# Values by seven half products instead of eight, with position copies, normalization and sums moved, in a two-layer attention kernel

## The chip, the cores and the metric

The kernel runs on one core of a Trainium2 chip. The metric is the device time of one execution in microseconds (us). Before the change it is 3358.13 us, the median of three runs (3357.68 to 3358.46).

A core has five engines that run side by side and meet through semaphores: PE (TensorE, matrix products into PSUM; its weight loads are listed as PEld), DVE (VectorE), ACT (ScalarE), POOL (GpSimd) and SP (SyncE, here only a queue that starts DMAs). Each engine works through its own instructions in order.

## The reference

Two layers, each on four images of 32 x 32 positions with 768 channels, 12 heads of 64:

```python
for layer in (0, 1):
    y = group_norm(x, groups=32)            # over positions and 24 channels
    q, k, v = heads(y @ Wqkv + bqkv)        # no bias in layer 0
    bias[h, w, k] = q . Rh  and  q . Rw     # relative positions, along rows and columns
    attn = softmax(scale * q k^T + bias)    # 1024 x 1024 per head
    x = x + (attn @ v) @ Wproj + bproj
```

Everything is float32. For one image the values are one product of a 1024 x 768 matrix (positions by channels) with a 768 x 768 matrix.

## The kernel before

**Units.** There are 8 (layer, image) rounds of 6 head pairs: 48 pairs, numbered g, `pair = g % 6`. A pair is worked in 8 steps n, one for each block of 128 query positions; a step is an iteration of the loop at L776. "Even" and "odd" are said of `pair`. Heads of a pair lie in the two halves of the 128 partitions, and most products use 64 partitions, so that two of them run in PE at the same time.

**One step.** The order of all instructions is written out by hand (`tc.manual_schedule`, L722); each engine's queue is that order cut to its own instructions. A step (g, n) issues: touches for half-done groups (see below); DMAs put off from earlier steps; `biases` two steps ahead (POOL, two passes of 1024 elements); `scores` one step ahead (PE, 8 records), then `exponentials` (DVE subtracts bias from score and takes the minimum, ACT exponentiates); the place copies of the positions; reading back transposed blocks (SP); then products of the next pair, `turn` (two DVE transposes and a store `td` to DRAM), `divide` one step ahead (DVE reciprocal, then ACT, in steps 2 and 4 half on POOL), and further products. In steps 6 and 2 `weigh` multiplies read-back attention blocks (`pt`) with values (`av`, 64 records); DVE copies the sum out.

**Groups of products.** Products of pair g + 1 run during the steps of pair g: G0 to G3 for queries and keys, V0 and V1 for values, O0 and O1 for the output projection. The plan at L769 says which are worked in which step; a group listed in two steps is done in two halves. `crossed` (L315) is such a group: in its first half each of two PSUM banks collects one partition half's products, in its second half the other's. Between them stands `between` (L311), one DVE instruction that rewrites one weight column, so that the second half waits for it and it for the first half. A group's results wait in PSUM in one of two buffers of pool `ps_m`; positions, weighted sums and output products use the same two.

**Queries and keys** are already computed by seven half-size products in place of eight: `combine` (L130) makes differences of weight blocks on POOL, `sums` (L282) differences of input blocks, and G0 to G3 the products, whose results are added by DVE.

**Values** come for two pairs at once (`project_values`, L392): for a double pair starting at an even g, four groups i of 256 positions, each by 24 matmuls with 256 output columns (both pairs' values), and ACT copies the results into the value tiles (L405), two copies a group. Groups 0 and 1 run in the odd pair before, 2 and 3 in the even pair itself. `combine_values` makes one weight difference that the input sums call for.

**Positions.** `positions` (L409) multiplies q with the position table (tile `tp`, 128 columns), ACT copies the result twice (L425, L428); it is called in step 2 and step 7, `place_positions` after the exponentials.

**Next image.** In pair 3 `norm` gathers the statistics and makes scale and shift through small DMAs (steps 1, 2, 4, 5, 7); `applies` says in which steps of pair 4 ACT normalizes which input blocks, `sum_steps` in which steps POOL makes the input sums.

Of the kernel before, what the change touches and what calls it, by code (L numbers as in the profile page):

```python
# [31 lines left out]
FP = mybir.dt.float32  # L32
AF = mybir.ActivationFunctionType
ALU = mybir.AluOpType
ENGINES = {getattr(mybir.EngineType, e) for e in ("PE", "DVE", "Activation", "Pool", "SP")}

P = 128
# [19 lines left out]
def attention_blocks(ctx: ExitStack, tc: tile.TileContext, a: dict, out: bass.AP):  # L57
# [63 lines left out]
    def load_wv(g):  # L121

        im, pair = divmod(g, NP)
        w = wpool.tile([P, NC, 2 * P], FP, tag="wv", name=f"wv_{g}")
        wv_of[g] = w
        nc.sync.dma_start(
            out=w, in_=a[f"wv{images[im][0]}"][pair // 2].rearrange("p (c o) -> p c o", c=NC)
        )
# [11 lines left out]

    def combine_values(g):

        w = wv_of[g]
        nc.gpsimd.tensor_tensor(w[:, NB:], w[:, NB:], w[:, :NB], ALU.subtract)

# [91 lines left out]
    def norm(im):  # L237
# [6 lines left out]
        back = dram2.tile([C, 2], FP, tag="back", name=f"back_{im}")  # L244
        g = small.tile([NG, 2, GS, 2], FP, tag="g", bufs=1, name=f"g_{im}")
        st = small.tile([NG, 2, 6], FP, tag="gst", bufs=1, name=f"gst_{im}")
# [6 lines left out]

        def by_group():
            queue.dma_start(out=g[:, 0, :, :], in_=per.rearrange("(g k) s -> g k s", k=GS))

        def groups():
            for k in range(2):
                nc.vector.bn_stats(st[:, k, :], g[:, 0, :, k])
                nc.vector.bn_aggr(mv[:, k, :], st[:, k, :])  # L260
            nc.vector.tensor_scalar(mv[:, 2, 0:1], mv[:, 0, 1:2], mv[:, 1, 0:1], EPS, ALU.add, ALU.add)
            nc.scalar.activation(mv[:, 2, 1:2], mv[:, 2, 0:1], AF.Sqrt)

        def inverses():
            nc.vector.reciprocal(mv[:, 2, 0:1], mv[:, 2, 1:2])
            nc.vector.tensor_scalar(mv[:, 2, 1:2], mv[:, 0, 0:1], mv[:, 2, 0:1], -1.0, ALU.mult, ALU.mult)
            for k in range(2):
                nc.vector.tensor_copy(g[:, 1, :, k], mv[:, 2, k : k + 1].to_broadcast([NG, GS]))
            queue.dma_start(out=back.rearrange("(g k) s -> g k s", k=GS), in_=g[:, 1, :, :])
# [31 lines left out]
    class Crossed:  # L301
# [8 lines left out]

        def between(self):  # L311
            x = self.last[:, 0:1]
            nc.vector.tensor_reduce(x, x, mybir.AxisListType.X, ALU.max)  # L313

    def crossed(t, pairs, two, kept=None):  # L315

        n = len(pairs)
        for half in range(2):
            for at in range(n):
                for h in range(2):  # L320
                    h = h ^ half
                    rows = ROWS[h ^ half]
                    to, w, x = two(t, pairs[n - 1 - at if half else at], h, rows)
                    nc.tensor.matmul(  # L324
                        to, lhsT=w, rhs=x, start=(half, at) == (0, 0), stop=(half, at) == (1, n - 1)
                    )
            if half == 0:
                yield kept if kept is not None else two(t, pairs[n - 1], 1, slice(0, P))[1]

# [61 lines left out]

    def project_values(g, i):  # L392

        im, pair = divmod(g, NP)
        xn, w = xn_of[im][i // 2], wv_of[g]
        if i == 0:
            for h in range(2):
                v_of[g + h] = vpool.tile([P, NT, P], FP, tag="v", name=f"v_{g + h}")
        t = ps_m.tile([P, 2, HALF], FP, tag="m", name=f"pv_{g}_{i}")
        yield from crossed(t, range(NC), lambda t, c, k, rows: (  # L400
            t[:, k, : 2 * P], xn[c][rows, (2 * (i % 2) + k) * P : (2 * (i % 2) + k + 1) * P],
            w[rows, c, :],
        ), w[:, NC - 1, :])
        for h in range(2):
            nc.scalar.copy(v_of[g + h][:, 2 * i : 2 * i + 2, :], t[:, :, h * P : (h + 1) * P])  # L405
        if i == 3 and g + 2 < NPAIR:
            later.append(lambda: load_wv(g + 2))

# [258 lines left out]
    def run(todo):  # L667
        while todo:
            todo.pop(0)()

    def prepare(g):

        first, i = (g - 1, 2) if g % 2 else (g, 0)
        groups = {f"G{kind}": Crossed(lambda kind=kind: products(g, kind)) for kind in range(4)}
        for k in range(2):
            groups[f"V{k}"] = Crossed(lambda k=k: project_values(first, i + k))
        return groups
# [15 lines left out]
    def take(groups, n):  # L693
# [15 lines left out]
    applies = {  # L709
        2: ((0, 0), (0, 1), (0, 2)), 3: ((0, 3),), 4: ((0, 4), (0, 5), (1, 0)),  # L710
        5: ((1, 3), (1, 1), (1, 4)), 7: ((1, 2), (1, 5)),
    }
    sum_steps = {
        (4, 5): ((3, 0),),
        (4, 6): ((1, 0), (2, 0), (3, 1)),
        (4, 7): ((1, 1), (2, 1)),
        (5, 0): ((3, 2), (1, 2), (2, 2)),
        (5, 1): ((4, 0),),
        (5, 2): ((4, 1), (4, 2)),
    }  # L720

    with tc.manual_schedule(engines=ENGINES):  # L722
# [16 lines left out]
        def both(*names):  # L739
            for name in names:  # L740
                now[name].part()
            for name in names:
                now[name].between()
            for name in names:
                now[name].part()
# [3 lines left out]
        run(placing)  # L749
        both("V1", "G1")  # L750
        later.pop(0)()
        combine_values(0)
        load_w(1, "a")
        now["G2"].part()
        now["G3"].part()
        now["G2"].between()
        now["G2"].part()
        positions(0, 1)()
# [9 lines left out]
        held = [ahead["G0"]]  # L768
        plan = {  # L769
            0: ("O1 previous", "G0", "V0"), 1: ("V0", "V1"), 3: ("V1", "G1"),  # L770
            4: ("G1", "G3", "G2"), 5: ("G2", "O0"), 7: ("O0", "O1", "G0 next"),
        }
        before = {}

        units = [(g, n) for g in range(NPAIR) for n in range(NT)]
        for at, (g, n) in enumerate(units):  # L776
# [37 lines left out]
            if at + 2 < len(units):  # L814
                biases(*units[at + 2])
            placing = [positions_of() for positions_of in (early_positions if n == 2 else ())]
            if n == 2:
                early_positions.clear()
            exps = scores(*units[at + 1]) if at + 1 < len(units) else None
            if n == 7 and g + 1 < NPAIR:  # L820
                placing.append(positions(g + 1, 1))
            if exps:
                exps()
            run(placing)
            run(behind[0])
            behind.append(behind.pop(0))
            if pair == 3 and n in stages and not end:
                stages[n]()
            pieces = [now[name] for name in plan.get(n, ()) if now.get(name)]
            if n == 0 and len(pieces) == 2:  # L830
# [11 lines left out]
            turn(g, n)  # L842
            run_part(1 if n == 0 else len(pieces))
            if at + 1 < len(units):
                divide(*units[at + 1])
            if n in (0, 1) and g + 1 < NPAIR:
                combine(g + 1, n)
            if n == 4 and pair % 2 and g + 1 < NPAIR:
                combine_values(g + 1)
            if pair == 4 and not end:  # L850
                for h, c in applies.get(n, ()):
                    apply(c, h)
            if not end:
                for which, c in sum_steps.get((pair, n), ()):
                    sums(im + 1, which, c)
            for k in range(2 if n == 0 else 1, len(pieces)):
                run_part(k)
# [68 lines left out]
```

## Time and profile before

| | value |
|---|---|
| median of three runs | 3358.13 us |
| the profiled execution | 3358.64 us |
| its span, first to last instruction | 3356.7 us |
| granted PE clock | 0.999 |
| L324 PE value products, 4608 records | mean 376 ns each |
| L420 PE position products, 1536 records | mean 272 ns each |
| L405 ACT value copies, 192 | 59.9 us, 361 ns each |
| L144 POOL value weight difference, 24 | 44.0 us, 1835 ns each |
| L133 POOL weight differences, 192 | some 1000 ns each |
| L313 DVE touches of wv, 96 | 13.9 us, 144 ns each |
| POOL sc waits for DVE tb | 603.7 us, 160 times |

A row of groups gives the line, the engine, the operation, the tile written and the tiles read, the shapes, the count, the busy time and the mean of one. A row in order of time gives the start, the length, and what ran. A row of waits gives who waited for whom, the total, how often, and the longest. Durations of single matmuls include their way through the array, so neighbours overlap; the time between the starts of two runs tells what a run costs. Idle time of an engine that nobody waits for costs nothing.

### The profile page before, as it was taken

What the parts mean: (1) busy time and instruction counts of PE and PEld (TensorE: products, weight loads), DVE (VectorE), ACT (ScalarE), POOL (GpSimd) and SP (SyncE); (2) the same over time, 40 slices, a digit from 0 to 9 for tenths busy, and PEclk for the clock granted to TensorE, in tenths of its full rate; (3) what the DMA queues carried; (4) which work ended last, traced back from release to release, by engine and by line L of the source; (5) the groups of instructions that cost most, each with busy time, mean ns of one, the idle gap of its engine ahead of it and who ended that gap; (6) DMA issues with size and microseconds to landing.
All of it is one profiled execution on the core that took longest, in us unless ns stands there. A gap on an engine that the chain in (4) does not pass through costs nothing.

```text
span 3356.7 us, 58091 instructions
## 1 busy us (share of the span) xinstructions
PE 3316.0 (99%) x21604; PEld 1874.7 (56%) x21604; DVE 2417.8 (72%) x3923; ACT 2041.0 (61%) x3140; POOL 2333.9 (70%) x1187
## 2 busy tenths in 40 slices
PE   6999999999999999999999999999999999999998
PEld 4555555555555555555555555555555555555554
DVE  4887777777787776777777776767776676767775
ACT  3666655566556665566656666566666566665563
POOL 6777866668666686667867668676686667766662
PEclk9999999999999999999999999999999999999999
DMA  3998989899899988998988999999988989898887
GB/s 129 319 331 311 331 308 335 315 327 327 318 323 319 324 315 309 317 326 312 324 310 314 329 313 324 312 326 313 329 311 309 328 309 334 305 319 299 311 290 270
DMA packets 524153, 1046.94 MB, mean 312 GB/s; under 512 B 139104, under 2 KB 202080, under 8 KB 474720
## 3 DMA queue, kind: packets, MB, share of 16 engines
q1 hardware_dynamic: 470976, 1015.84, 85.8%
q10 hardware_dynamic: 52896, 27.40, 2.7%
q8 instruction: 171, 2.80, 0.3%
q14 instruction: 110, 0.90, 0.1%
HBM read 568.00 MB, written 475.09 MB: 311 GB/s over the span
## 4 chain that ended last, share of the span: by engine, by line
PE 95%; DMA 3%; DVE 1%; issue 0%; ACT 0%; SPq 0%; POOL 0%; ACTq 0%; DVEq 0%
PE pj L324 21%; PE av L547 19%; PE s L482 19%; PE pv L324 15%; PE oo L324 13%; PE pj L352 3%; PE tp L420 3%; DMA td<-tb 2%; PE o L626 1%; DMA xn<-in_x 1%; DVE tb L518 1%; DMA pt<-td 1%; DVE st L201 0%; DVE sc L494 0%; POOL sc L468 0%
## 5 line engine op out<-in xcount | busy, mean ns | idle before, releaser
L468 POOL TENSOR_TENSOR sc<-rel 128x1024 f32<-128x1024 f32 x768 | 1880.1, 2478 | 634.9 <-DVE tb L518 603.7
L494 DVE CUSTOM_DVE_ANT_0 sc<-s,sc 128x1024 f32<-128x1024 f32 x768 | 911.1, 1226 | 531.2 <-PE s L482 464.0
L498 ACT ACTIVATE sc<-sc,sm 128x1024 f32<-128x1024 f32 x768 | 878.8, 1146 | 498.2 <-DVE sm L494 497.2
L512 ACT ACTIVATE sc<-sc,sm 128x1024 f32<-128x1024 f32 x674 | 743.0, 1143 | 564.8 <-DVE sm L506 437.5
L518 DVE STREAM_TRANSPOSE tb<-sc 128x1024 f32<-128x1024 f32 x768 | 909.9, 1227 | 36.7 <-DMA td<-tb 35.2
L482 PE MATMUL s<-k,q 64*128 64x512 f32 x3072 | 738.6, 596 | 2.7 <-DVE sm L494 2.7
L547 PE MATMUL av<-pt,v 128*64 128x256 f32 x6144 | 685.3, 381 | 6.5 <-DMA pt<-td 5.5
L547 PEld LDWEIGHTS av<-pt,v 128*64 128x64 f32 x6144 | 434.4, 137 | 286.6 <-issue 44.0
L324 PE MATMUL pv<-wv,xn 64*128 64x256 f32 x4608 | 522.8, 376 | 1.0 <-DVE wv L313 1.0
L324 PEld LDWEIGHTS pv<-wv,xn 64*128 64x128 f32 x4608 | 446.9, 187 | 114.2 <-issue 54.5
L324 PE MATMUL oo<-attn,wo 64*128 64x512 f32 x2112 | 475.3, 589 | 0.0
L482 PEld LDWEIGHTS s<-k,q 64*128 64x128 f32 x3072 | 289.2, 187 | 316.2 <-issue 291.7
L324 PEld LDWEIGHTS oo<-attn,wo 64*128 64x128 f32 x2112 | 200.9, 187 | 228.0 <-issue 227.1
L510 POOL TENSOR_SCALAR sc<-sc,sm 128x1024 f32<-128x1024 f32 x94 | 105.5, 1122 | 303.2 <-DVE sm L506 298.2
L324 PE MATMUL pj<-xn,wa 64*128 64x512 f32 x1152 | 268.1, 596 | 4.4 <-DVE wa L313 2.9
L324 PE MATMUL pj<-xn,w 64*128 64x512 f32 x1152 | 263.3, 589 | 1.6 <-DVE w L313 1.6
L324 PE MATMUL pj<-s,w 64*128 64x512 f32 x576 | 262.5, 589 | 0.0
L324 PE MATMUL pj<-s,wc 64*128 64x512 f32 x576 | 262.5, 589 | 0.0
L324 PEld LDWEIGHTS pj<-xn,wa 64*128 64x128 f32 x1152 | 113.4, 189 | 140.3 <-issue 126.6
L324 PEld LDWEIGHTS pj<-xn,w 64*128 64x128 f32 x1152 | 111.6, 187 | 137.4 <-issue 134.9
L443 ACT COPY rel<-raw 32x256 f32<-32x256 f32 x384 | 155.1, 404 | 16.2 <-DMA rel<-tdr 5.5
L324 PEld LDWEIGHTS pj<-s,wc 64*128 64x128 f32 x576 | 107.7, 187 | 67.4 <-issue 67.4
(86 smaller groups left out, 2127.1 us busy)
## 6 DMA issues: line engine op xcount, KB each, us to landing
td<-tb SPq DMA_DIRECT2D x384, 1024.0 KB, 6.1
pt<-td SPq DMA_DIRECT2D x382, 1024.0 KB, 8.9
tdr<-t ACTq DMA_DIRECT2D x96, 256.0 KB, 6.1
part<-res SPq DMA_DIRECT2D x84, 256.0 KB, 4.2
res<-part SPq DMA_DIRECT2D x84, 256.0 KB, 4.8
wa<-in_wqk SPq DMA_DIRECT2D x48, 384.0 KB, 3.2
wc<-in_wqk SPq DMA_DIRECT2D x48, 384.0 KB, 5.6
wv<-in_wv SPq DMA_DIRECT2D x24, 768.0 KB, 12.5
```

Of the source, the lines that this page charges most:

```text
L324: nc.tensor.matmul(to, lhsT=w, rhs=x, start=(half, at) == (0, 0), stop=(half, at) == (1, n - 1))
L352: nc.tensor.matmul(t[:, h, :], lhsT=w[rows, c, :], rhs=x[c][rows, :], start=(c == 0), stop=(c == NB - 1),)
L420: nc.tensor.matmul(ps[:, h, j, :], lhsT=q[rows, at * P : (at + 1) * P], rhs=tabs[l][rows, :], start=True, stop=True,)
L443: nc.scalar.copy(rel[rows, :, 0, :, :], raw[rows, :, :, WIDE - 1 - HW - y : WIDE - 1 - y])
L468: nc.gpsimd.tensor_tensor(sc.rearrange("p (a k) (u l) -> p a (k u) l", a=4, l=8), rel[:, h, 0, m, :].unsqueeze(1).unsqueeze(3).to_broadcas ...
L482: nc.tensor.matmul(ps[h][:, cols], lhsT=q[rows, n * P : (n + 1) * P], rhs=k[rows, cols], start=True, stop=True,)
L494: nc.vector.tensor_tensor_reduce(out=sc, in0=ps[h], in1=sc, scale=-scale, scalar=BIG, op0=ALU.add, op1=ALU.min, accum_out=st[:, 0, h : h + 1],
L498: nc.scalar.activation(sc, sc, AF.Exp, bias=st[:, 0, h : h + 1], scale=-1.0, accum_out=st[:, 1, h : h + 1],)
L510: nc.gpsimd.tensor_scalar(sc, sc, st[:, 2, h : h + 1], 1.0, ALU.mult, ALU.mult)
L512: nc.scalar.mul(sc, sc, st[:, 2, h : h + 1])
L518: nc.vector.transpose(tb[:, :, h, :], sc_of[g, n, h])
L547: nc.tensor.matmul(av[rows, at * 2 * P : (at + 1) * 2 * P], lhsT=v_of[g][:, k, rows], rhs=pt_of[g, quarter].rearrange("p n r k h i -> p (n ...
```

## The change

Values of a double pair are made by seven half-size products. The value weights are cut into four blocks (by channel half and by pair), the inputs into four (by channel half and by position half). Group kind 0 multiplies raw weights with the first position half; POOL then replaces blocks by differences, in two stages, and kinds 1 to 3 use these with the input sums that queries and keys use already. Kinds 0, 1 and 2 are crossed groups of 48 matmuls with 128 output columns, kind 3 a single part of 24. Results are added up in the value tiles: one ACT copy and nine DVE additions a double pair. Kinds 0 and 3 run in the odd pair, 1 and 2 in the even one, and the plan differs between them: in odd pairs V1 (kind 3) stands after G1 in step 3. The position copies of step 2 go to the end of step 1, ahead of the division there. In step 3 of even pairs the touch is an ACT copy ahead of the division. Normalization and input sums start one step earlier, and the group statistics lie in the buffer of the position copies.

```diff
-    def combine_values(g):
-        w = wv_of[g]
-        nc.gpsimd.tensor_tensor(w[:, NB:], w[:, NB:], w[:, :NB], ALU.subtract)
+    def combine_values(g, stage):
+        w, t2 = wv_of[g]
...
+        if stage == 0:
+            sub(w11, w12, w11)
+            sub(w12, w22, w12)
+        else:
+            sub(t2, w22, w11)
+            sub(w21, w21, t2)
...
+            window = tmppool.tile([P, 2, 4, WIDE], FP, tag="raw", name=f"g_{im}")
...
-        def between(self):
+        def between(self, scalar=False):
             x = self.last[:, 0:1]
+            if scalar:
+                nc.scalar.copy(x, x)
+                return
...
-        t = ps_m.tile([P, 2, HALF], FP, tag="m", name=f"pv_{g}_{i}")
-        yield from crossed(t, range(NC), lambda t, c, k, rows: (
-            t[:, k, : 2 * P], xn[c][rows, (2 * (i % 2) + k) * P : (2 * (i % 2) + k + 1) * P],
-            w[rows, c, :],
-        ), w[:, NC - 1, :])
-        for h in range(2):
-            nc.scalar.copy(v_of[g + h][:, 2 * i : 2 * i + 2, :], t[:, :, h * P : (h + 1) * P])
+        t = ps_m.tile([P, 2, 4, P], FP, tag="m", name=f"pv_{g}_{kind}")
+        if kind == 3:
+            for b in blocks:
+                for c in range(NB):
+                    for h, rows in enumerate(ROWS):
+                        nc.tensor.matmul(
+                            t[:, h, b, :], lhsT=s4[c][rows, b * P : (b + 1) * P], rhs=w22[rows, c, :],
...
+            ops = {
+                0: ((w11, x0), (w21, x0[NB:])),
+                1: ((w2, s2), (w12, s3)),
+                2: ((w11, x1), (w21, x1[NB:])),
+            }[kind]
+            yield from crossed(t, [(b, c) for b in blocks for c in range(NB)], lambda t, bc, h, rows: (
+                t[:, h, bc[0], :], ops[h][1][bc[1]][rows, bc[0] * P : (bc[0] + 1) * P],
+                ops[h][0][rows, bc[1], :],
+            ), 2)
...
+        if kind == 0:
+            nc.scalar.copy(y10, ts[0])
+            add(y00, ts[1], y10)
+        elif kind == 3:
+            add(y01, ts[0], y10)
+            add(y01, ts[1], y01)
+        elif kind == 1:
+            add(y11, ts[0], y10)
+            add(y01, ts[0], y01)
+            add(y11, ts[1], y11)
+        else:
+            add(y10, ts[1], y11)
+            add(y01, ts[0], y01)
+            add(y11, ts[0], y11)
...
-        2: ((0, 0), (0, 1), (0, 2)), 3: ((0, 3),), 4: ((0, 4), (0, 5), (1, 0)),
-        5: ((1, 3), (1, 1), (1, 4)), 7: ((1, 2), (1, 5)),
+        1: ((0, 0), (0, 3)), 2: ((0, 1), (0, 4)), 3: ((1, 0), (1, 1), (0, 2)),
+        4: ((1, 3), (1, 4), (0, 5)), 5: ((1, 2), (1, 5)),
...
-        both("V1", "G1")
+        both("G1", "G2")
         later.pop(0)()
-        combine_values(0)
+        for stage in range(2):
+            combine_values(0, stage)
         load_w(1, "a")
-        now["G2"].part()
         now["G3"].part()
-        now["G2"].between()
-        now["G2"].part()
+        now["V1"].part()
...
-        plan = {
-            0: ("O1 previous", "G0", "V0"), 1: ("V0", "V1"), 3: ("V1", "G1"),
-            4: ("G1", "G3", "G2"), 5: ("G2", "O0"), 7: ("O0", "O1", "G0 next"),
-        }
+        same = {
+            0: ("O1 previous", "G0", "V0"), 4: ("G1", "G3", "G2"), 5: ("G2", "O0"),
+            7: ("O0", "O1", "G0 next"),
+        }
+        plans = {**same, 1: ("V0", "V1"), 3: ("V1", "G1")}, {**same, 1: ("V0",), 3: ("G1", "V1")}
...
+            done = 2 if n == 0 else len(pieces) if n == 1 or (n, pair % 2) == (3, 0) else 1
+            for k in range(1, done):
+                run_part(k)
+            if n == 1:
+                placing = [positions_of() for positions_of in early_positions]
+                early_positions.clear()
+            if (n, pair % 2) == (3, 0):
+                for group in held:
+                    group.between(scalar=True)
+                held = []
             if at + 1 < len(units):
                 divide(*units[at + 1])
...
-            if n == 4 and pair % 2 and g + 1 < NPAIR:
-                combine_values(g + 1)
+            if n in (3, 5) and pair % 2 and g + 1 < NPAIR:
+                combine_values(g + 1, n // 4)
```

## The prediction

> **What bounds the kernel now.** I read the page's engine line first, then the answer for three stretches of the span, then who made TensorE (PE) wait, then its groups by shape and one stretch in order of time.
>
> ```profile
> PE 3316.0 (99%) x21604; PEld 1874.7 (56%) x21604; DVE 2417.8 (72%) x3923; ACT 2041.0 (61%) x3140; POOL 2333.9 (70%) x1187
> ```
> ```profile
> 233.00:3271.00 3038.00, 3036.62 (x19966) 1718.96 (x19966) 2207.38 (x3580) 1884.93 (x2901) 2147.72 (x1081) 1.00 0.90 318
> 0.00:233.00 233.00, 204.03 (x1316) 121.17 (x1316) 159.33 (x269) 127.41 (x203) 163.50 (x98) 0.99 0.73 251
> ```
> ```profile
> PE groups L216 <- DVE nrm L215: 15.0, 1, 15.0
> PE av L547 <- DMA pt<-td: 5.5, 5, 1.7
> PE pj L324 <- DVE wa L313: 2.9, 2, 2.3
> ```
> ```profile
> 1003.81 2.76 PE L324 MATMUL pv<-wv,xn 64*128 64x256 f32 x24
> 1006.40 1.88 PE L482 MATMUL s<-k,q 64*128 64x512 f32 x8
> 1008.12 5.35 PE L324 MATMUL pv<-wv,xn 64*128 64x256 f32 x48
> 1013.30 1.06 PE L420 MATMUL tp<-tab,q 64*128 64x128 f32 x16
> 1014.19 1.89 PE L482 MATMUL s<-k,q 64*128 64x512 f32 x8
> 1016.00 7.13 PE L547 MATMUL av<-pt,v 128*64 128x256 f32 x64
> ```
> From 233 to 3271 us PE is busy 3036.62 of 3038.00 us at full clock (the columns after the length are PE, PEld, DVE, ACT and POOL busy, clock, DMA share, GB/s). So the time is PE's own work plus a head and a tail, and any change must be priced in PE time and in new PE waits. DVE, POOL and the DMA engines (share 0.90) come next and matter only where they make PE wait.
>
> **The unit of PE work.** Each fp32 matmul leaves two records, and matmuls on the two halves of the partitions run at the same time; two concurrent records are one slot below. The time from the start of one run to the next gives its price: 24 records of 256 columns take 1006.40 - 1003.81 = 2.59 us, 12 slots of 216 ns; 16 records of 128 columns (the position products, the only ones of that width) take 1014.19 - 1013.30 = 0.89 us, 8 slots of 111 ns, say 111.5. All of these load new weights in every slot, as the new products do.
>
> **Part 1, the values.** Per double pair (two head pairs) four groups of 24 matmuls of 256 columns go: 96 slots x 216 = 20.74 us. Three groups of 48 and one of 24 matmuls of 128 columns come: 168 slots x 111.5 = 18.73 us. That is 2.01 us less of the bounding engine, all of it in the odd pair (three runs of 24 slots in place of four of 12), while each of the four runs in the even pair grows from 2.59 to 2.68 us. Times 23 double pairs in the loop: -46.2 us. The slot price is bounded below by half of the 216 ns slot (108: -60 us). Above, it is less sure: a slot is four PE records (two weight loads, two matmuls), 28 ns each at 111.5, and the trace holds that pace for 8 slots only, where the new runs have 24 to 48 slots plus the position products. Its longest dense stretches (the 256-column runs) go at 54 ns a record, which would make a slot 216 ns and the kernel 168 x 216 - 20.74 = +15.5 us a double pair, +373 us. I take 111.5, since the eight slots are evenly paced also where PE had waited just before (the position products at 55.1 us).
>
> The Trainium skill ("TensorE: Matmul & The Clock Gate", Back-to-back issue gap) speaks against the change here: a steady stream of weight load and matmul pairs, it says, is held to about 81 ns per matmul at 128 columns, more than the columns alone. By it a slot of two would be 162 ns and the change an estimated +6.5 us a double pair, +155 us; the trace's row beside it is 111 ns for the same kind of slot, in runs of 8.
>
> **Part 2, what follows the products.** ACT loses 8 copies of 361 ns and gains one of 585 per double pair. DVE gains 9 adds of 512 elements from PSUM, at 0.69 us (the row of the same add for k): 6.2 us a double pair, 149 us in all, 72% to some 78%; one DVE touch of 0.14 us a double pair goes. PE pays only where it waits for them. The rows:
> ```profile
> 1009.58 1.22 DVE L494 CUSTOM_DVE_ANT_0 sc<-s,sc 128x1024 f32<-128x1024 f32 x1
> 1010.72 2.37 DVE L518 STREAM_TRANSPOSE tb<-sc 128x1024 f32<-128x1024 f32 x2
> 1013.01 0.12 DVE L506 RECIPROCAL sm<-sm 128x2 f32<-128x2 f32 x1
> ```
> Even pair, step 1: the first value group ends at 1010.97 (24 slots from 1008.12, plus the last one's 0.27), three adds end near 1013.0, and the position products, which take the freed PSUM buffer, are due at 1013.48 after the second group's 24 slots. 0.4 us to spare: 0; without that second group the full 2 us would show. Odd pair, step 1: the copy waits on ACT for the exponentials (they end 4.0 us after the second slot run begins, 943.40 in the pair before) and the add follows, to 944.7; the buffer's next user is the weighted sum at 944.9: 0 to 0.2. Even pair, step 3: three adds, 1.9 us, now stand before the transposes, and the next scores' subtraction is due 0.4 us after the reciprocal: 0, or 0.5 late where statistics (0.9 us) stand there too, and hidden by the 2.57 us of k products. Odd pair, step 3: two adds end with the next scores' arrival: 0. Also there, value kind 3 takes a PSUM buffer between G1 and G3, which costs G3 a wait for two adds (1.6 us, 24 times: +38) if the buffer just freed is given out, and nothing if the older one is. In the old stretch the second value group follows the first without a gap though the copies out of the first end at 1012.73, so the older is given out: 0.
>
> What the DVE adds do delay is the transposes of steps 1 and 3, by some 2.1 to 2.7 us, and on SP's queue everything behind their store:
> ```profile
> 1029.88 0.33 SPq L520 DMA_DIRECT2D td<-tb  x1
> 1030.32 8.67 SPq L454 DMA_DIRECT2D rel<-tdr  x8
> 1039.08 0.38 SPq L119 DMA_DIRECT2D wa<-in_wqk  x1
> 1039.56 0.93 SPq L529 DMA_DIRECT2D pt<-td  x2
> 1040.58 0.46 SPq L520 DMA_DIRECT2D td<-tb  x1
> ```
> ```profile
> DMA to landing us min/median/max: 5.1/8.9/12.8
> ```
> The second read-back lands at about 1040 + 8.9 = 1048.9 and is wanted halfway through the weighted sum, 1051.7. 2.1 us later leaves 0.7 us at the median and a wait of 3.2 at the slowest landing: 0 to 2.1 a pair, I take 0.2. Then the store behind it (1040.58) is late as well, and the transposes two steps on wait for its landing (35.2 us, 22 times, now); behind them on DVE stands the copy that frees the buffer of the next position products, about 1 us ahead of need (1055.95 to 1057.05). 0 to 1 a pair, I take 0.15. Both together: 24 x 0.35 = +8 us, bounds 0 and +50 (24 x 2.1).
>
> **Part 3, the moves.** The position copies go ahead of a division in ACT's queue. The weight load of the weighted sum waits for them 34.9 us in 46 times now, but PE's own list has no such wait, so it gains 0; the division behind them (ACT, one of 1.14 us) waits for the later reciprocal anyway. One touch per even pair moves from DVE to ACT (0.2 us, behind the exponentials, ahead of a division that is not due yet): 0. Combining the value weights: one POOL pass of 1.84 us becomes four of 1.0, in two later steps with several us of POOL idle before the next biases: 0; if POOL were late, the scores' subtraction would be, by up to 1 us. Normalization (12 ACT passes of 0.80 us an image) and sums (12 on POOL of 1.28) start a step earlier, the scale's read having been issued 37 us before its first use now (711.79 to 748.92), still some 28 after: 0, at most 1 us in 7 images. The window that shares the position buffer makes its small read on SP wait for the place copies, with a transposed store queued behind it: under 1 us, 7 times, off the path: 0.
>
> **The head.** From 33.78 to 55.12 us PE does value, query and key groups with two waits (1.58 and 1.17 us) before the second position products. New: four half groups of 2.57, G3 2.57 and kind 3 at 2.68 = 15.5 against 21.3 us, less 0.5 for the wider even runs: -5.3 if nothing else is late. POOL's combine is 2.2 us longer there and the first read-backs already hold PE up: bounds -5.5 and 0, I take -3.
>
> **Sum.** Profiled execution 3358.64 (span 3356.7 and 1.9 around it); -46.2 - 3 + 8 = 3317.4. The median of the runs is 0.5 below the profiled one: 3317.
>
> **Rivals.**
> A, on the other side: PE cannot be fed 128-column slots for that long. For it: no row shows more than 8 in a row. Against: the even pace of those 8, also after a wait. It decides at a slot price of 20.74 / 168 = 123 ns; at 54 ns a record it ends at 3358.6 + 373 = 3732, halfway (164 ns) at about 3525. Chance 0.14.
> B: DVE's lateness is paid in full in each even pair, through the read-back or the buffer: 3317 - 8 + 50 = 3359, or half of it, 3335. For it: the 0.7 us left over; against: a PE wait lets the transfers catch up, and in most pairs the landing is at the median. Chance 0.15, split evenly around 3351.
> C: no new wait, and the whole head: 3358.6 - 46.2 - 5.3 = 3307. Chance 0.06.
> Forecast as summed, 3303 to 3335: 0.65.
>
> **How the numbers follow.** A measurement tells about 0.2%, 6.7 us, from no change. Faster: 0.65 + 0.06 + half of B, 0.08 = 0.79. Same: 0.05 of B and near A's threshold. Slower: 0.16. Range 3302 to 3365: it takes in C's 3307, the forecast and B's 3359, and leaves A out (0.14).
>
> **What would show it.** Right: value matmul records 8064 in place of 4608, mean 272 ns, a 24-slot run near 2.68 us; PE still 99% busy; DVE up by some 145 us and ACT down by some 45. Wrong: value runs of 48 records longer than 2.9 us (A); PE waiting for pt<-td or a value add, or ACT's position copy, some 24 times and by over 1 us (B). The prediction falls if PE's idle time in the loop passes 20 us.

## The result, and the profile after

| | before | after |
|---|---|---|
| median of the runs compared | 3358.3 us (3357.68 to 3359.33) | 3317.65 us (3316.78 to 3318.15) |
| the profiled execution | 3358.64 us | 3317.58 us |
| its span | 3356.7 us | 3315.3 us |
| granted PE clock | 0.999 | 0.999 |

The changed kernel takes 0.9878 of the time before (95% interval 0.9861 to 0.9895), four runs of each. The forecast was 3317.

First the engine line of the page of the changed kernel, and two stretches of its span, the head and the loop (start and end, length; busy time and instructions of PE, PEld, DVE, ACT, POOL; clock; DMA share; GB/s).

```profile
PE 3270.6 (99%) x25060; PEld 1882.7 (57%) x25060; DVE 2549.7 (77%) x4091; ACT 1999.1 (60%) x2996; POOL 2386.5 (72%) x1259
```

```profile
0.00:233.00 233.00, 205.26 (x1646) 126.41 (x1648) 173.87 (x288) 128.94 (x197) 173.01 (x106) 0.99 0.74 262
233.00:3230.00 2997.00, 2990.35 (x23096) 1721.76 (x23092) 2325.17 (x3728) 1841.84 (x2763) 2191.18 (x1145) 1.00 0.91 321
```

PE is still the bound: in the loop it is idle 6.65 of 2997 us, where it was idle 1.38 of 3038. DVE has gained 132 us and ACT lost 42, as the sum had it to within 13 and 3 us.

The waits of PE (who waited for whom, total us, times, longest us):

```profile
PE groups L224 <- DVE nrm L223: 14.6, 1, 14.6
PE av L599 <- DMA pt<-td: 9.0, 8, 2.2
PE pj L341 <- DVE wa L330: 3.5, 2, 3.0
```

The first, in the head, is the old one (15.0). The wait for the read-back, 5.5 us before, is 9.0. No row is a wait for the position copies, and the rows of waits for value additions come to 0.8 us in all.

The value products and what follows them, from the groups kept apart by shape (count | busy us, mean ns of one | idle us before it):

```profile
L341 PE MATMUL pv<-wv,xn 64*128 64x128 f32 x4608 | 274.1, 272 | 1.0 <-DVE wv L330 1.0
L341 PE MATMUL pv<-wv,s 64*128 64x128 f32 x2304 | 136.5, 272 | 0.0
...
L426 PE MATMUL pv<-wv,s 64*128 64x128 f32 x1152 | 68.4, 272 | 0.0
```

```profile
L443 DVE TENSOR_TENSOR v<-pv,v 128x512 f32<-128x512 f32 x216 | 140.2, 686 | 61.0 <-ACT v L445 44.0 <-PE pv L341 10.2 <-PE pv L426 5.9
```

That makes 4608 + 2304 + 1152 = 8064 records of 272 ns, and 216 additions of 686 ns, both as foretold. What the records cost is read in order of time, here in an even pair (g = 16, start, length, what ran):

```profile
1129.31 2.85 PE L341 MATMUL pv<-wv,s 64*128 64x128 f32 x48
1131.98 2.85 PE L341 MATMUL pv<-wv,xn 64*128 64x128 f32 x48
1134.66 1.06 PE L472 MATMUL tp<-tab,q 64*128 64x128 f32 x16
1135.56 1.89 PE L534 MATMUL s<-k,q 64*128 64x512 f32 x8
```

From start to start, 24 + 24 + 8 slots take 1135.56 - 1129.31 = 6.25 us, or 111.6 ns a slot. The 224 records of weight loads and matmuls in it go at 27.9 ns each, without a slower second half.

**Where the time went.** Whole pairs are measured from the start of the first scores of one to those of the next:

| | before | after | times | together |
|---|---|---|---|---|
| odd pair, undisturbed | 68.72 us | 66.40 us | 23 | -53.4 |
| even pair | 68.72 us | 69.08 us | 24 | +8.6 |
| extra time in five odd pairs | | | | +8.7 |
| head, to the second scores | 60.63 us | 55.33 us | 1 | -5.3 |
| sum | | | | -41.4 |

The difference of the spans is -41.4 as well. The extra time lies in pairs 7, 13, 19 and 25 (pair 1 of images 1 to 4: 1.1, 2.9, 2.1 and 1.9 us) and in pair 5 (0.7). In these five pairs PE has six waits, 6.6 us of idle time together: four for the read-back (4.4 us) and two before position products (2.2 us). From start to start each of the six costs 0.17 us more than its idle time; the last 1 us lies in gaps too short for a row.

### The profile page after: what moved, and what is told of

The parts are those of the page before. It is cut to its first block, busy times and chain, and to the rows that moved or that the text cites. A ratio compares the mean times of both kernels' runs of the same rounds, so it can differ in the third digit from the quotient of the medians.

```text
span 3315.3 us, 64963 instructions
## 1 busy us (share of the span) xinstructions
PE 3270.6 (99%) x25060; PEld 1882.7 (57%) x25060; DVE 2549.7 (77%) x4091; ACT 1999.1 (60%) x2996; POOL 2386.5 (72%) x1259
## 4 chain that ended last, share of the span: by engine, by line
PE 90%; DMA 5%; DVE 2%; POOL 1%; issue 1%; SPq 0%; ACT 0%; ACTq 0%; DVEq 0%; POOLq 0%
PE pj L341 21%; PE s L534 19%; PE av L599 18%; PE oo L341 13%; PE pv L341 11%; PE pj L369 3%; DMA td<-tb 3%; PE tp L472 2%; PE pv L426 2%; DMA pt<-td 1%; DMA xn<-in_x 1%; DVE tb L570 1%; PE o L678 1%; POOL sc L520 1%; DVE st L209 0%
## 5 line engine op out<-in xcount | busy, mean ns | idle before, releaser
L341 PEld LDWEIGHTS pv<-wv,xn 64*128 64x128 f32 x4608 | 271.6, 188 | 35.2 <-issue 25.1
L341 PE MATMUL pv<-wv,xn 64*128 64x128 f32 x4608 | 274.1, 272 | 1.0 <-DVE wv L330 1.0
L443 DVE TENSOR_TENSOR v<-pv,v 128x512 f32<-128x512 f32 x216 | 140.2, 686 | 61.0 <-ACT v L445 44.0
```

The source lines that it names most:

```text
L341: nc.tensor.matmul(to, lhsT=w, rhs=x, start=at == half == 0, stop=at == 0 and half == 1)
L443: add = lambda to, x, y: nc.vector.tensor_tensor(to, x, y, ALU.add)
```

## The experiments

The question was no longer whether PE becomes faster, which the rows above settle, but which of the priced-at-nothing moves were needed, and what the 8.7 us are. Every kernel below is the changed one with an edit, unless said otherwise. "Over after" is the distance to 3317.65; the median of the kernel before lay between 3357.5 and 3359.1 beside each of them.

| kernel | median us | ratio to before, 95% | over after |
|---|---|---|---|
| e1_copies_late | 3359.38 | 1.0003 (0.9994 to 1.0013) | +41.7 |
| e2_copies_alone | 3358.56 | 0.9999 (0.9990 to 1.0009) | |
| e3_norm_late | 3335.17 | 0.9930 (0.9913 to 0.9946) | +17.5 |
| e4_touch_dve | 3331.04 | 0.9913 (0.9898 to 0.9928) | +13.4 |
| e10_values_alone | 3369.61 | 1.0030 (1.0020 to 1.0041) | +52.0 |
| e8_kind3_first | 3323.83 | 0.9896 (0.9881 to 0.9911) | +6.2 |
| e5_no_adds | 3311.66 | 0.9858 (0.9843 to 0.9872) | -6.0 |
| e6_loads_pair2 | 3316.22 | 0.9874 (0.9860 to 0.9889) | -1.4 |
| e7_short_stats | 3313.28 | 0.9864 (0.9849 to 0.9878) | -4.4 |
| e9_loads_apart | 3316.80 | 0.9877 (0.9862 to 0.9892) | -0.9 |
| e0_changed_again | 3320.08 | 0.9884 (0.9868 to 0.9901) | +2.4 |

### The position copies behind the division again

```diff
+            if n == 2:
+                placing = [positions_of() for positions_of in early_positions]
+                early_positions.clear()
             exps = scores(*units[at + 1]) if at + 1 < len(units) else None
...
-            if n == 1:
-                placing = [positions_of() for positions_of in early_positions]
-                early_positions.clear()
```

> The changed kernel with one move undone: the position copies of step 2 stand behind the division of step 2 again. The prediction priced this move at 0, since PE never waited for these copies before: that reading gives the changed kernel's 3317.65 us, within 3. Against it: the value adds now make the reciprocal late. In an even pair of the changed kernel the reciprocal ends at 1136.41 us, the division at 1137.6, the two copies would then end near 1138.6, and the weighted sum, which takes their PSUM buffer, starts at 1137.37: some 1.4 us of PE wait in each of 23 even pairs, more (1.5) in pair 4 of an image, where two normalizations stand in front as well: +35 to +46 us, and PE's waits would name ACT raw.

Measured: 3359.38 us. The whole gain is gone, by one edit that moves two ACT copies of 0.6 and 0.4 us behind one ACT pass. The waits of PE in this kernel have a row that the changed one lacks:

```profile
PE av L599 <- ACT raw L480: 32.2, 23, 2.4
```

Three engines in order of time, in step 1 and 2 of an even pair of this kernel; first DVE, then ACT, then PE:

```profile
1010.28 1.89 DVE L443 TENSOR_TENSOR v<-pv,v 128x512 f32<-128x512 f32 x3 [0.21 <-PE pv L341]
1012.08 2.36 DVE L570 STREAM_TRANSPOSE tb<-sc 128x1024 f32<-128x1024 f32 x2
1014.37 0.12 DVE L558 RECIPROCAL sm<-sm 128x2 f32<-128x2 f32 x1
```

```profile
1014.52 1.15 ACT L564 ACTIVATE sc<-sc,sm 128x1024 f32<-128x1024 f32 x1 [3.13 <-DVE sm L558]
1015.57 0.56 ACT L477 COPY t<-tp 128x512 f32<-128x512 f32 x1
1016.04 0.40 ACT L480 COPY raw<-tp 128x288 f32<-128x288 f32 x1
```

```profile
1012.74 1.06 PE L472 MATMUL tp<-tab,q 64*128 64x128 f32 x16
1013.64 1.89 PE L534 MATMUL s<-k,q 64*128 64x512 f32 x8
1016.49 3.88 PE L599 MATMUL av<-pt,v 128*64 128x256 f32 x33 [0.97 <-ACT raw L480]
```

The chain is read downwards. Three value additions stand before the transposes, the transposes before the reciprocal, and ACT cannot divide without the reciprocal. So ACT idles for 3.13 us, and the copies of positions that had long been ready wait behind the division. The weighted sum takes the PSUM buffer that these copies empty. It starts at 1016.49, right after the copies (1016.44), 0.97 late. In the kernel before, the same chain had room; ACT there:

```profile
1013.17 1.15 ACT L512 ACTIVATE sc<-sc,sm 128x1024 f32<-128x1024 f32 x1 [0.44 <-DVE sm L506]
1014.40 0.59 ACT L425 COPY t<-tp 128x512 f32<-128x512 f32 x1
1014.88 0.41 ACT L428 COPY raw<-tp 128x288 f32<-128x288 f32 x1
```

The copies end at 1015.29 and the weighted sum starts at 1016.00. The first copy waits there for its own products (1013.30 + 1.06 = 1014.36), not for the division. Counted from the reciprocal, which starts at 1013.01, the copies need 2.07 us (1016.44 - 1014.37 here) and could have ended at 1015.08, so the reciprocal had 0.92 us of room. That is less than the 1.89 us that the additions take; the rest is the 0.97 us.

Even pairs take 70.12 us in place of 69.08: 24 x 1.04 = 25 us. Pair 4 of seven images loses 1.4 to 3.1 us more, 18 together. There the normalization's passes stand in ACT's queue ahead of the copies as well, as ACT's order in pair 4 of image 2 shows:

```profile
1151.04 1.15 ACT L564 ACTIVATE sc<-sc,sm 128x1024 f32<-128x1024 f32 x1 [3.18 <-DVE sm L558]
1152.10 1.50 ACT L290 ACTIVATE xn<-xn,nrm 128x512 f32<-128x512 f32 x2
1153.51 0.56 ACT L477 COPY t<-tp 128x512 f32<-128x512 f32 x1
1153.97 0.39 ACT L480 COPY raw<-tp 128x288 f32<-128x288 f32 x1
```

The weighted sum starts behind them at 1154.41, after a wait of 2.37 us, 1.40 more than in the other even pairs. Over seven pairs that is 9.8 of the 18 us. The other 8.4 are PE's clock: in five of the seven pairs it was granted at half for 3.41 us, beginning 0.3 to 1.3 us after the wait. These five lose 3.08 us, the two without it 1.40. The stretch in pair 4 of image 2 (length; busy time and instructions of PE, PEld, DVE, ACT, POOL; clock; DMA share; GB/s):

```profile
1155.60:1159.01 3.41, 3.41 (x20) 1.91 (x18) 1.29 (x3) 3.35 (x7) 3.41 (x2) 0.50 0.98 317
```

So a wait of PE can cost more than its own length. The changed kernel has no such stretch from 65 us to its last two, though one wait in between (to 167.65) lasts 2.24 us. Why some waits are followed by one and others are not stays open.

### The position copies moved in the kernel before

The kernel before, with this move alone: step 1 works its second value half first, then copies, then divides.

```diff
-            placing = [positions_of() for positions_of in (early_positions if n == 2 else ())]
-            if n == 2:
-                early_positions.clear()
...
+            if n == 1:
+                for k in range(1, len(pieces)):
+                    run_part(k)
+                pieces = []
+                placing = [positions_of() for positions_of in early_positions]
+                early_positions.clear()
             if at + 1 < len(units):
                 divide(*units[at + 1])
```

> The kernel before with one part of the change alone: the position copies at the end of step 1, ahead of the division. Nothing in its PE list waits for them: 3358.3 us, within 2. If they did hold PE unseen (the weight load of the weighted sum waits for them 34.9 us in all): up to 35 less.

Measured: 0.9999 of before, all pairs at 68.72 us. The prediction's "gains 0" is right for the old kernel: the move is worth nothing there and 42 us beside the additions (some 8 of them by the clock).

### Normalization and sums one step later again

```diff
-        1: ((0, 0), (0, 3)), 2: ((0, 1), (0, 4)), 3: ((1, 0), (1, 1), (0, 2)),
-        4: ((1, 3), (1, 4), (0, 5)), 5: ((1, 2), (1, 5)),
+        2: ((0, 0), (0, 1), (0, 2)), 3: ((0, 3),), 4: ((0, 4), (0, 5), (1, 0)),
+        5: ((1, 3), (1, 1), (1, 4)), 7: ((1, 2), (1, 5)),
...
-        (5, 0): ((2, 2),),
-        (5, 1): ((4, 2),),
+        (5, 0): ((3, 2), (1, 2), (2, 2)),
+        (5, 1): ((4, 0),),
+        (5, 2): ((4, 1), (4, 2)),
```

> The changed kernel with normalization and input sums of the next image back at the steps of before. The prediction priced this move at 0, at most 1 us in each of 7 images: 3317.65 us, within 3. The other reading: the value group of kind 3 in pair 5, step 3, needs the last input sums, which POOL would now make one to two steps later, and waits for them: over 1 us in 7 images, +7 us or more, with PE waiting for POOL s.

Measured: +17.5 us. Pair 5 of every image that has a successor now takes 2.2 to 4.2 us more than an odd pair should; the two longest, 4.2 and 3.9, again hold 3.41 us at half clock. The place, first PE and then POOL in order of time (step 3 of pair 5 of image 0):

```profile
400.57 0.39 PE L426 MATMUL pv<-wv,s 64*128 64x128 f32 x4
401.91 0.49 PE L426 MATMUL pv<-wv,s 64*128 64x128 f32 x4 [0.95 <-POOL s L310]
403.15 2.50 PE L426 MATMUL pv<-wv,s 64*128 64x128 f32 x40 [0.74 <-POOL s L310]
```

```profile
395.76 4.87 POOL L520 TENSOR_TENSOR sc<-rel 128x1024 f32<-128x1024 f32 x2
400.60 2.49 POOL L310 TENSOR_TENSOR s<-xn,s 128x512 f32<-128x512 f32 x2
403.06 4.87 POOL L520 TENSOR_TENSOR sc<-rel 128x1024 f32<-128x1024 f32 x2
```

Value kind 3 takes input sum 4. With the old table its last two parts are made on POOL only from 400.60, in the step in which PE wants them at 400.57. The old kernel had no product in this place that needed that sum. So the move has a job that the prediction did not see when it compared only the times at which inputs and scale are read.

### The touch on DVE

```diff
-            if (n, pair % 2) == (3, 0):
-                for group in held:
-                    group.between(scalar=True)
-                held = []
```

Without these lines DVE makes the touch at the head of step 4.

> The changed kernel with the touch of step 3 of even pairs on DVE at the head of step 4, as before, in place of ACT. The prediction priced this at 0. But in the changed kernel the reciprocal of step 3, behind which the touch would stand, ends at 1153.35 us and the second half of that key group starts at 1153.23, so the touch (0.14 us) and its way to PE would hold it some 0.45 us in 23 even pairs, 0.9 more in the six where statistics stand in between: +10 to +16 us, PE waiting for DVE wc. If something else hides it: 0.

Measured: +13.4 us, within what was expected. Even pairs take 69.42 us, 0.34 more, and 0.6 to 0.9 more again where statistics stand in between. One such place, DVE and then PE in order of time:

```profile
1024.46 0.12 DVE L558 RECIPROCAL sm<-sm 128x2 f32<-128x2 f32 x1
1024.51 0.67 DVE L209 BATCH_NORM_STATS2 st<-xn 128x6 f32<-128x512 f32 x1
1025.21 0.21 DVE L212 BATCH_NORM_AGGREGATE mv<-st 128x2 f32<-128x12 f32 x1
1025.34 0.11 DVE L330 TENSOR_REDUCE wc<-wc 128x1 f32<-128x1 f32 x1
```

```profile
1025.50 0.69 PE L341 MATMUL pj<-s,wc 64*128 64x512 f32 x1 [0.88 <-DVE wc L330]
```

A touch of 0.11 us holds PE, since it stands behind additions, transposes, reciprocal and statistics in DVE's queue.

### The values without the three moves

The three edits above together: what is left is the seven half products, their additions, the plan by parity and the head.

> The changed kernel with all three moves undone together: position copies in step 2, normalization and sums at the steps of before, the touch of step 3 of even pairs on DVE. What is left is the seven half products, their adds and the plan by parity. If the three single losses add up (41.7, 17.5 and 13.4 us above 3317.65, against different waits): 3383 to 3395 us, slower than the kernel before by some 30. If they cover one another (a PE that waits once finds the next thing ready): 3360 to 3375. By the prediction's zeros: 3318.

Measured: 3369.61 us, 1.0030 of before (eight runs against eleven): slower than before, by some 12 us. Of PE's waits in it:

```profile
PE av L599 <- ACT raw L480: 22.4, 23, 1.0
PE pv L426 <- POOL s L310: 12.3, 14, 1.2
PE av L599 <- DMA pt<-td: 8.9, 8, 2.2
PE pj L341 <- DVE wc L330: 4.6, 6, 0.9
```

Each of the three waits that the single edits opened is there. The moves are worth 52.0 us together, less than the 72.6 of the single losses. The difference has a place: the wait for the copies is 1.0 us at most here and 2.4 in the first experiment, for pair 4 has no extra time where the normalization does not begin in step 1. That is 18 of the 20.6 us, the half clock in it included. Even pairs take 70.47 us, 69.08 + 1.04 + 0.35.

### Kind 3 ahead of G1

```diff
-        plans = {**same, 1: ("V0", "V1"), 3: ("V1", "G1")}, {**same, 1: ("V0",), 3: ("G1", "V1")}
+        plans = {**same, 1: ("V0", "V1"), 3: ("V1", "G1")}, {**same, 1: ("V0",), 3: ("V1", "G1")}
```

> The changed kernel with value kind 3 ahead of G1 in step 3 of odd pairs, so that its two DVE adds (1.4 us) stand before the transposes of that step. PE does the same work. If the new waits of the changed kernel (8.7 us in five odd pairs, where a read-back lands after PE wants it) hang on how early the transposed store of step 3 is issued, 1.4 us later makes these five longer by 1.4 each and adds some in the pairs with under 1.4 us to spare: +8 to +15 us. If the store is held by the transfers in front of it anyway: within 3 us of 3317.65.

Measured: +6.2 us, in neither of the expected ranges and not by the way expected. The wait for the read-back did not grow; another did:

```profile
PE av L599 <- DMA pt<-td: 7.7, 7, 1.5
PE pj L341 <- DVE wc L330: 6.7, 11, 1.2
```

With kind 3 first, G1's half ends the step and its touch falls to the head of step 4, behind DVE's other work, as in the touch experiment. The edit was meant to test the read-back and tested the touch.

### What the remaining 8.7 us are

Four kernels take away one suspected cause each. In the first, ACT copies take the raw products and the additions are left out:

```diff
-            add(y00, ts[1], y10)
+            nc.scalar.copy(y00, ts[1])
         elif kind == 3:
-            add(y01, ts[0], y10)
-            add(y01, ts[1], y01)
+            nc.scalar.copy(y01, ts[0])
```

(likewise in kinds 1 and 2).

> The changed kernel without its value adds: each value group's result is taken by one ACT copy (kind 0 by two), so eight half products are not put together and DVE has as little to do for the values as before the change; PE's work is unchanged. Leaves out: the additions that complete the values. Rival (DVE's lateness makes the new waits): the 8.7 us of waits in odd pairs go, 3309 us, within 2. Theory (the odd pair asks for the same transfers in 2.3 us less): they stay for the most part, 3314 to 3319 us.

Measured: 3311.66 us, between the two expectations, with DVE at 2414.6 us, 135 less. The values are left incomplete. Odd pairs keep 5.0 us of extra time.

The second puts the loads of the next image's inputs into pair 2 (and with them the statistics of these inputs, which follow the loads by two steps in images 0 to 2), the third keeps them in pairs 1 and 2 but out of steps 2 to 5:

```diff
-    loads = {(1, 0): 0, (1, 2): 1, (1, 4): 2, (1, 6): 3, (2, 0): 4, (2, 2): 5}
+    loads = {(2, n): n for n in range(6)}
```

```diff
-    loads = {(1, 0): 0, (1, 2): 1, (1, 4): 2, (1, 6): 3, (2, 0): 4, (2, 2): 5}
+    loads = {(1, 0): 0, (1, 1): 1, (1, 6): 2, (1, 7): 3, (2, 0): 4, (2, 1): 5}
```

> The changed kernel with the six input loads of the next image (256 KB each) all in pair 2, steps 0 to 5, in place of four in pair 1 and two in pair 2. Theory (transfers): the waits in pair 1 of images 1 to 4 (8.0 of the 8.7 us) go and pair 2, an even pair with more time, takes the loads: 3310 us, within 3. Rival (DVE): loads don't matter where DVE's result statistics stay: 3317, within 3.

> The changed kernel with the six input loads of the next image at steps 0, 1, 6, 7 of pair 1 and 0, 1 of pair 2, so that none is issued in steps 2 to 5, where the read-back that PE waits for is on its way. If the waits come from those loads together with DVE's lateness: the 8.0 us in pair 1 go and pair 2 gets none, 3309 to 3312 us. If the loads only shift the waits to other pairs, as with all six in pair 2: 3314 to 3318.

Measured: in the second kernel the extra time of odd pairs falls to 0.9 us, but even pairs (12, 16 and 20) gain 3.5, and pair 2 of image 0 takes 7.7 us more than in the changed kernel: there one wait for the read-back is 4.8 us long, and the clock is at half for 6.83 us from 232.2 us on. The profiled execution, at 3321.02, is the longest of its four. So the median is that of the second reading (3317), while the waits leave pair 1 as the first reading had it. In the third, 8.6 us of extra time remain in odd pairs, 7.4 of them in pair 1: the median lies in the second range, but the waits did not shift to other pairs as that reading had it.

The fourth takes the statistics of the results over 32 of 512 columns, so most of them are left out:

```diff
-            stats(im + B, o, i, to)
+            stats(im + B, o, i, to[:, :32])
```

> The changed kernel with the statistics of layer 0's results taken over 32 of 512 columns, which takes some 0.6 us off each of 48 DVE instructions (in pairs 0 to 2 of images 1 to 4, steps 7 and 0). Leaves out: most of the statistics for layer 1's normalization. Rival (DVE's lateness): the four waits in pair 1 of images 1 to 4 go, 3309 to 3311 us. Theory (transfers): these statistics stand in steps 7 and 0, four steps from the late read-back, and the waits stay, 3315 to 3319 us.

Measured: 3313.28 us, between the two expectations; in the profiled execution (3311.86) the extra time of odd pairs is 0.4 us.

Last, the changed kernel once more, for how far it agrees with itself:

> The changed kernel itself, on the chip of the next run: 3317.65 us, within 3, with some 9 us of extra time in single odd pairs as in its first profile. If the extra time were a matter of one execution, other pairs would show it and its sum would differ by more than half.

Measured: 3320.08 us, single executions from 3314.01 to 3323.02. The extra time is again mostly in pair 1 of images (7: 1.6, 13: 2.5, 25: 1.6), 6.4 us in odd pairs and 1.3 in an even one. So the place holds, while the amount varies by several us. Differences under some 6 us, those of the last four edits, are therefore not settled by time.

What follows, from single profiles: the waits belong to pair 1, where input loads stand on SP's queue and statistics on DVE's, and they need both. Without most of the statistics 0.4 us are left, against 8.7 and 6.4; and in the changed kernel itself pair 1 of images 5 and 6 has the same four loads, no statistics, and no extra time. With the loads in pair 2, pair 1 has no extra time either, but in that profile other pairs lose as much or more. At which steps of pairs 1 and 2 the loads stand does not matter much (8.6 us). Most of the time stays without the additions (5.0 us), so they are not needed for it. How loads and statistics together delay the read-back is open. The form of the wait itself is plain in the profile of the changed kernel, in pair 13; SP, then DVE, then PE in order of time:

```profile
957.18 0.93 SPq L581 DMA_DIRECT2D pt<-td  x2
958.21 4.72 SPq L572 DMA_DIRECT2D td<-tb  x2
```

```profile
970.78 2.37 DVE L570 STREAM_TRANSPOSE tb<-sc 128x1024 f32<-128x1024 f32 x2 [5.04 <-DMA td<-tb]
973.07 0.12 DVE L558 RECIPROCAL sm<-sm 128x2 f32<-128x2 f32 x1
973.12 0.67 DVE L608 COPY attn<-av 128x512 f32<-128x512 f32 x1
```

```profile
966.78 3.67 PE L599 MATMUL av<-pt,v 128*64 128x256 f32 x32 [0.93 <-DMA pt<-td]
970.38 1.99 PE L534 MATMUL s<-k,q 64*128 64x512 f32 x8
973.84 1.16 PE L472 MATMUL tp<-tab,q 64*128 64x128 f32 x16 [1.47 <-DVE wo L330]
```

The second read-back, issued at 957.18, holds the second half of the weighted sum for 0.93 us. The store behind it lands late, the transposes wait 5.04 us for it, and the copy that empties the weighted sum's buffer, behind them, ends at 973.79; the position products that take the buffer start at 973.84, 1.47 late. (The row names the touch of wo, the next instruction on DVE, which ends 0.05 us behind the copy.)

## Why the prediction was right, point by point

- **The price of a slot** (111.5 ns, from eight slots): right, 111.6 over 56 slots in one stretch. The step "20.74 - 18.73 = 2.01 us a double pair" measured 2.32 - 0.36 = 1.96. With 23 odd and 24 even pairs that is -44.8 us, 1.4 less than the -46.2 forecast.
- **Rival A** (PE cannot be fed for so long) fell, with the 54 ns a record that it took from the 256-column runs: the runs of 48 to 112 matmuls keep 27.9 ns. The Trainium skill's figure of about 81 ns per matmul at 128 columns ("TensorE: Matmul & The Clock Gate", Back-to-back issue gap) would have made a run of 24 slots an estimated 3.9 us; the row is 2.67 us. Where page and row differ here, the row decides, for this form of product: two fp32 matmuls at a time on 64 partitions each.
- **What hides the additions.** Even pair, step 1: the additions end at 1134.08 and the position products start at 1134.66, without a wait; 0.4 us to spare were forecast, 0.6 are there. The older PSUM buffer is given out, as read from the old stretch: G3 has no wait of 1.6 us, and 38 us are not lost.
- **The new waits**: +8 forecast, 8.7 measured, but the place was wrong. The prediction spread 0.35 us over 24 even pairs, through the lateness that the additions cause there; even pairs show none (69.08 is 68.72 and the 0.36 of wider runs). They are in pair 1 of images, for the most part, and reach PE by the two ways the prediction describes: the read-back itself (4.4 us of idle time), and store, transposes, buffer (2.2). That the sum agrees is luck, since the reason given for it, the additions, is not what most of them hang on: 5.0 us stay without any addition.
- **The head**: -3 taken between -5.5 and 0, -5.3 measured; this term was sized too cautiously. POOL's longer combine, which was to take part of it, made PE wait nowhere: in the old head PE waited 1.58 us for a touch and 1.17 for the addition of q before the second position products, in the new one only 0.60 for a value addition.
- **DVE and ACT**: +145 and -45 forecast, +132 and -42 measured. The 216 additions overlap by some 37 ns each, so they are busy for 140 and not 149 us.
- **The moves**, all priced at 0. As terms of the sum they stand, since the sum priced the additions with the moves in place. As a statement of what they are worth the zeros are wrong by 41.7, 17.5 and 13.4 us, 52 together. The position copies are the plainest: the sentence "PE's own list has no such wait, so it gains 0" looked at the old waits only. The prediction held the additions of 1.9 us and the rows of the reciprocal (1013.01) and of the weighted sum (1016.00), between which the division and both copies have to fit, and did not lay one on the other.
- **Rivals B and C.** B's sign, PE waiting for the position copy some 24 times, is what the first experiment shows (23 times, 32.2 us): it is the kernel without the move. C, no new wait at all, is 10 us below the result.
- **The chances.** "Slower 0.16" does not follow from the list: only A (0.14) ends slower, and B's half that is not faster, 0.07, ends the same.

## What to carry to other kernels

When work is put in front of an in-order engine's late instruction, list everything that waits for that instruction on other engines, and everything queued behind those waiters; a copy that frees a PSUM buffer should not stand behind a pass that waits for another engine. A reorder that gains nothing alone may be the condition under which a saving on the bounding engine arrives: here a gain of some 40 us is a loss of 12 without three moves, of which the one that was tried alone in the kernel before, the position copies, gains nothing there (the other two were not tried there). And a forecast of waits should be tested by where they fall (which pair, which step), since a total can agree for the wrong reason.

## What was not expected of the hardware

- PE took weight loads and matmuls of 128 columns on alternating partition halves at 27.9 ns a record for 224 records in a row, while the kernel before had shown that pace for 32 records only.
- Waits of PE of some 2.4 us were followed in five of seven cases by 3.41 us at half clock, 1.7 us more of PE's time each (pair 4 in the first experiment); after the 2.24 us of the changed kernel no such stretch came.
- The DVE copy of the 32 x 24 group statistics (14 times) went from 188 to 574 ns on average. Its new target is not what takes the time: 6 of the 14 still take 159 to 161 ns. The 8 slow ones, 797 to 1041 ns, all run beside a POOL pass and end 27 to 34 ns after it, mostly after the first difference of the value weights, which the change has moved into that step. Pair 3 of image 1, DVE and then POOL:

```profile
687.16 0.87 DVE L282 COPY g<-gmv 32x24 f32<-32x24 f32 x1
```

```profile
686.92 1.08 POOL L144 TENSOR_TENSOR wv<-wv 128x384 f32<-128x384 f32 x1
```

  The one slow copy of the kernel before (522 ns) ends 42 ns after a POOL pass too. That the copies wait for these passes is read from where they end; no experiment tried it. PE waits for none of them.
- Executions of the changed kernel spread from 3314.01 to 3323.02 us on one chip (four), against 3356.01 to 3360.20 of the kernel before beside it (seven). Beside another experiment the kernel before spread as far, from 3354.22 to 3362.20 (thirteen), so that the changed kernel is less steady is not shown.
